# Attention of a DiT block: four key chunks to a group, one PSUM ring, and group sums added in SBUF

## The chip, the cores and the metric

One core of a Trainium2 chip runs the whole program. The metric is device time in microseconds (us), the median of several runs; less is better. Everything is computed in fp32.

## The reference

A transformer block with conditioning, for B = 2 sequences of N = 2048 tokens, C = 576 features, 16 heads of 36:

```python
mod = silu(c) @ w_ada + b_ada                     # six vectors of 576 per sequence
sh_msa, sc_msa, g_msa, sh_mlp, sc_mlp, g_mlp = split(mod, 6, axis=1)
xn = ln(x) * (1 + sc_msa) + sh_msa
q, k, v = (xn @ w_qkv + b_qkv) by head
q, k = ln(q) * qn_g + qn_b, ln(k) * kn_g + kn_b   # over the 36 of a head
o = softmax(q @ k.T * 36**-0.5) @ v
x = x + g_msa * (o @ w_proj + b_proj)
xn2 = ln(x) * (1 + sc_mlp) + sh_mlp
x = x + g_mlp * (gelu(xn2 @ w1 + b1) @ w2 + b2)
```

## The kernel before

For each sequence the program makes q, k and v (`inputs`), runs attention (`attend`) and the output projection (`outputs`); the MLP of both follows. Gains and biases of q and k are measured at run time, and where they are small enough (they are here) the softmax needs no maximum: exp of the scores, a product with v that has a column of ones beside it, and a division by that column's sum.

**A step of attention.** Two heads form a pair (8 pairs, `p`), 512 queries a block (4 blocks, `qb`), and one step (`g`, 8 per block) takes two key chunks of 128: chunk `g` of the first half of the keys and of the second. `scores` (L956) multiplies keys and queries. A head has 36 features; the first 32 lie in `km` and `qm`, in a strip of 32 rows for each of the four (head, half) combinations, which run side by side in TensorE; the last 4 lie in `ke` and `qe`, each four times, split into a high and a low part (`parted`, L761 and L762 on VectorE), and add a second, smaller product in the same strips. Two tiles `s` of two PSUM banks each result, ScalarE takes their exp into `pt` (L960, four buffers), and `values` (L968) multiplies with v: 128 rows by 64 columns, head 0 in one half of the columns and head 1 in the other. The scores of a step are issued ahead of the values of the step before. All of TensorE's instructions stand in the order in which the code is written.

**PSUM.** In attention the eight banks are three `s` tiles and two single-bank `acc` tiles. The values of a query block's eight steps add up in one `acc`.

**The end of a block** (`finish`). VectorE copies `acc` to `ot` (L980). Row 36 of each head holds the denominators: they go to DRAM (`den_dram`, L984) and come back to 64 partitions each (`den`, L985). VectorE takes the reciprocal (L986), multiplies (L987), and two to five DMAs put the result over the queries in `qo` (L992).

**The loads.** `take_q` copies the next block's queries from `qo` to `qm` and `qe`: 4 to 6 and 16 DMAs (L750 and L753, the same lines for keys). In the second block of each pair `take_k` does so for the next pair's keys. All these DMAs are issued by SP, in one queue. In attention the order on SP, ScalarE and VectorE is a scheduler's, which places instructions by its own estimates; what it has placed is fixed when the program is built. Each engine and each queue then goes through its own list in order.

**Hooks** put other work between the steps: the last two token tiles of `inputs`, and for the first sequence the rest of the modulation (`ada_...`).

Of the kernel before, what the change touches and what calls it, by code (L numbers as in the profile page):

```python
# [16 lines left out]
P = 128  # L17
# [14 lines left out]
def dit_block(  # L32
# [165 lines left out]
    def feature_biases(pool, pair, queue):  # L198

        bb = pool.tile([P, PART], F32, name="fb", bufs=1)  # L200
        nc.gpsimd.memset(bb, 0.0)
        for i, r, f, n in row_parts(pair):
            b_j = b_ada[pair[i] * C : (pair[i] + 1) * C]
            queue.dma_start(out=bb[r, n], in_=b_j[f].partition_broadcast(B))
        nc.vector.tensor_scalar_add(bb[0:64, :], bb[0:64, :], 1.0)
        return bb

    def feature_rows(pool, was, bb):
        ps = ada_rows(was)
        rows = pool.tile([P, 384], F32, name="rows", bufs=1)  # L210
        nc.vector.tensor_tensor(rows[:, :PART], ps, bb, ALU.add)
        nc.vector.tensor_tensor(rows[:, PART:], ps[:, 256:PART], bb[:, 256:PART], ALU.add)
        return rows
# [12 lines left out]
    def gates(pool, was, pair, whichs, bias_ins):  # L226

        bb = pool.tile([P, PART], F32, name="bb", bufs=1)
        pb = pool.tile([P, PART], F32, name="pb", bufs=1)
        nc.gpsimd.memset(bb, 0.0)  # L230
        nc.gpsimd.memset(pb, 0.0)
        parts = [*row_parts(pair)]
        for i, r, f, n in parts:
            b_j = b_ada[pair[i] * C : (pair[i] + 1) * C]
            nc.sync.dma_start(out=bb[r, n], in_=b_j[f].partition_broadcast(B))
            nc.sync.dma_start(out=pb[r, n], in_=bias_ins[i][f].partition_broadcast(B))
        ps = ada_rows(was)
        nc.vector.tensor_tensor(bb, ps, bb, ALU.add)
        nc.vector.tensor_tensor(pb, bb, pb, ALU.mult)
        for i, r, f, n in parts:  # L240
            nc.sync.dma_start(out=gate_dram[whichs[i], :, f], in_=bb[r, n])
            nc.sync.dma_start(out=gate_dram[whichs[i] + 1, :, f], in_=pb[r, n])
# [370 lines left out]
    def block_of_any():  # L613
        gains_by_partition()
        with tc.tile_pool(name="ada_later", bufs=2) as ada:
            gates(ada, ada_weights(ada, GATES[0]), *GATES)
            later = feature_biases(ada, LATER[0], nc.sync)
            features(feature_rows(ada, ada_weights(ada, LATER[0]), later), LATER[1])
# [83 lines left out]
    def block_of_small():  # L702
# [40 lines left out]

        def rows_taken(main, ends, halves, first, src, dst):

            for c in halves:
                for h in range(2):
                    r0 = 32 * (2 * c + h)
                    for i, row, d, n in head_rows(first + h * HD, DIMS):
                        nc.sync.dma_start(out=main[r0 + d : r0 + d + n, dst], in_=chunk(i, src(c))[row : row + n, :])  # L750
                    ((i, row, _, n),) = head_rows(first + h * HD + DIMS, HD - DIMS)
                    for j in range(4):
                        nc.sync.dma_start(  # L753
                            out=ends[r0 + n * j : r0 + n * j + n, dst], in_=chunk(i, src(c))[row : row + n, :]
                        )

        def parted(ends, rows, low, sign):

            for a in range(ends.shape[1] // BLK):
                part = ends[rows, a * BLK : (a + 1) * BLK]  # L760
                nc.vector.tensor_scalar(high[rows, :], part, sign[rows, :], None, ALU.mult)  # L761
                nc.vector.scalar_tensor_tensor(  # L762
                    part.bitcast(F32R), part, low[rows, :], high[rows, :].bitcast(F32), ALU.mult, ALU.add
                )

        def take_k(p):
# [3 lines left out]
            parted(e, slice(0, P), low_k, sign_k)  # L770

        def take_k_block(blk):

            c, a = divmod(blk, NBLK // 2)
            dst = slice(a * BLK, (a + 1) * BLK)
            src = lambda c: slice(blk * BLK, (blk + 1) * BLK)
            rows_taken(km[0], ke[0], (c,), C, src, dst)
# [44 lines left out]
        def inputs(b, weights, work, xnt, loaded):  # L822

            wq, wq4, bq = weights
            normed, squares, taken = {}, {}, []

# [33 lines left out]
            def by_feature(t, banks, all_on_vector=False):  # L860
# [17 lines left out]
                if t % TPB == TPB - 1:  # L878
                    if t == TPB - 1:
                        taken.append(take_q(0, 0))  # L880
                    taken.append(take_k_block(t // TPB))
                    if t == NT - 1:
                        taken.pop()()
# [6 lines left out]
            for t in range(NT):  # L890
                both = work.tile([P, 2 * C], F32, name="both", bufs=3)
                for w in range(3):
# [25 lines left out]
                    if w == (1 if t % 2 == 0 else 0):  # L918
                        if t + 1 < NT:
                            ahead = input_by_feature(b, rows)  # L920
                        if t >= 2:
                            by_feature(t - 2, [bank for ps in (s_tile(), s_tile()) for bank in (ps[:, 0], ps[:, 1])])
# [11 lines left out]
            def last(t, spare):  # L934
                ps = s_tile()
                by_feature(t, [spare, ps[:, 0], ps[:, 1]], True)

            return last

        NG = NT // 2  # L940

        def attend(b, pool, hooks):
# [3 lines left out]

            def scores(p, qb, g):
                i, j = p % 2, qb % 2
                keys = slice(g * P, (g + 1) * P)
                tiles = [s_tile() for c in range(2)]  # L950
                for k, q, first in ((km[i], qm[j], True), (ke[i].bitcast(F32R), qe[j].bitcast(F32R), False)):
                    for c in range(2):
                        for h in range(2):
                            r0 = 32 * (2 * c + h)
                            r = slice(r0, r0 + (DIMS if first else 4 * (HD - DIMS)))
                            nc.tensor.matmul(tiles[c][:, h, :], k[r, keys], q[r, :], start=first, stop=not first)  # L956
                pts = []
                for ps in tiles:
                    pt = pool.tile([P, 2, BLK], F32, name="pt", bufs=4)
                    nc.scalar.activation(pt, ps, AF.Exp, scale=SCALE)  # L960
                    pts.append(pt)
                return pts

            def values(p, acc, pts, g):
                for c, pt in enumerate(pts):
                    for h in range(2):
                        v0 = ((g + c * NT // 2) * H + 2 * p + h) * HV
# [4 lines left out]
                            start=(g == 0 and c == 0),  # L972
                            stop=(g == NG - 1 and c == 1),
                        )

            def finish(p, qb, acc):


                ot = pool.tile([P, BLK], F32, name="ot", bufs=2)
                nc.vector.tensor_copy(ot, acc)  # L980
                den = pool.tile([P, BLK], F32, name="den", bufs=2)
# [4 lines left out]
                nc.vector.reciprocal(den, den)  # L986
                nc.vector.tensor_tensor(ot, ot, den, ALU.mult)  # L987
                cols = slice(qb * BLK, (qb + 1) * BLK)
                for h in range(2):
                    for c, row, d, n in head_rows((2 * p + h) * HD):  # L990
                        for r in (row,) if c < FULL else (row, row + 64):
                            nc.sync.dma_start(  # L992
                                out=qo[r : r + n, c, cols], in_=ot[64 * h + d : 64 * h + d + n, :]
                            )

            steps = [(p, qb, g) for p in range(NPAIR) for qb in range(NBLK) for g in range(NG)]
            behind = None
            for p, qb, g in [*steps, (None, None, None)]:
                pts = None if p is None else scores(p, qb, g)
                if (p, qb, g) in hooks:  # L1000
                    hooks[p, qb, g]()
                if g == 3 and (p, qb) != (NPAIR - 1, NBLK - 1):
                    take_q(*((p, qb + 1) if qb + 1 < NBLK else (p + 1, 0)))()
                if g == 4 and qb == 1 and p + 1 < NPAIR:
                    take_k(p + 1)
                if behind is not None:
                    bp, bqb, bg, bpts = behind
                    if bg == 0:
                        acc = acc_tile()
                    values(bp, acc, bpts, bg)  # L1010
                    if bg == NG - 1:
                        finish(bp, bqb, acc)
                behind = (p, qb, g, pts)

# [79 lines left out]
        for b in range(B):  # L1094
# [5 lines left out]
            close_psum()  # L1100
            close_psum = opened_psum(a=2, s=3)
# [4 lines left out]
            def spare_taken():  # L1106
                opening["spare"] = acc_tile()

            def last_inputs_done():
                last_inputs(NT - 1, opening["spare"])  # L1110
                close_work()

            def ada_opened():
                opening["ada"], opening["close"] = opened("ada_later", 2, side="right")
                opening["was"] = ada_weights(opening["ada"], GATES[0])

            def ada_gates():
                gates(opening["ada"], opening["was"], *GATES)
# [10 lines left out]
            def output_opened():  # L1129
# [3 lines left out]
                (0, 0, 0): spare_taken,  # L1133
                (0, 0, 1): lambda: last_inputs(NT - 2, opening["spare"]),
                (0, 0, 2): last_inputs_done,
                (4, 0, 2): output_opened,
            }
            if b == 0:
                hooks |= {
                    (0, 2, 2): ada_opened,  # L1140
                    (1, 0, 4): ada_gates,
                    (2, 0, 4): ada_feature_rows,
                    (2, 0, 6): ada_features,
                }
            attend(b, att, hooks)
            close_att()
            close_psum()
            close_psum = opened_psum(s=4)
# [354 lines left out]
```

## Time and profile before

| | |
|---|---|
| median of 3 runs | 3381.02 us (3376.55 to 3383.67) |
| the profiled execution | 3382.14 us, span 3380.3 us, granted TensorE clock 0.993 |
| attention, first sequence (268 to 1101 us of the span) | TensorE busy 826 of 833, ScalarE 496, VectorE 204 |
| attention, second sequence (1423 to 2244 us) | TensorE busy 817 of 821, ScalarE 494, VectorE 200 |
| L968 values | 4096 instructions, busy 996.2 us |
| L956 scores | 4096 with `qm` and 2048 with `qe`, busy 592.3 and 419.9 us |
| L986 reciprocal | 64, 3353 ns each; idle ahead of them 752.9 us, ended by `den` landing |
| L980 copy | 64, 691 ns each |

A line of the profile names the source line, the engine, the operation and its tiles (out<-in). Matmuls overlap, so their busy times and mean durations are not costs; the distance between starts in the timeline is. An fp32 product appears as two instructions (two passes). For a DMA the profile has the time for which its queue issued it, not its flight; that it has landed shows in who goes on. "Idle before" is the engine's idle time ahead of an instruction, with what ended it.

### The profile page before, as it was taken

To read this page: it belongs to the slowest core of one execution; us is meant where nothing else is said; L and a number is where in the kernel's file an instruction comes from. 1 tells how busy PE (TensorE), PEld (TensorE's weight loads), DVE (VectorE), ACT (ScalarE), POOL (GpSimd) and SP (SyncE) were. 2 spreads that over 40 slices of the span, in tenths; PEclk is the share of its full clock that TensorE was granted. 3 is DMA by queue.
4 is the path that set the end of the run, shared out by engine and by line. 5 is a ranking of instruction groups with operands and counts; after the bars stand their busy time and mean duration, and the time that the engine had idled before them with its cause. 6 is when DMAs were issued, how large, how long until landed. Compare 5 with 4: busy or idle time off the path is not lost.

```text
span 3380.3 us, 46567 instructions
## 1 busy us (share of the span) xinstructions
PE 3318.8 (98%) x18143; PEld 1839.6 (54%) x18143; DVE 1313.8 (39%) x1877; ACT 1439.7 (43%) x1928; POOL 258.8 (8%) x249
## 2 busy tenths in 40 slices
PE   8999999999999999999999999998999999999998
PEld 5773333333333777633333333347888888777776
DVE  4663222222222366612222222226445443544554
ACT  2335555666666033356666666632545453000000
POOL 1110000000000111100000000022000000111111
PEclk9999999999999999999999999999999999999999
DMA  3112212212111401111111111135322222433321
GB/s 125 27 28 60 68 48 61 54 40 52 42 45 35 138 24 29 32 42 42 41 41 38 41 41 43 34 113 184 120 84 83 87 83 75 172 121 116 130 98 36
DMA packets 122996, 234.25 MB, mean 69 GB/s; under 512 B 22279, under 2 KB 64848, under 8 KB 120720
## 3 DMA queue, kind: packets, MB, share of 16 engines
q1 hardware_dynamic: 111800, 193.10, 18.7%
q0 software_dynamic: 10240, 36.61, 3.2%
q8 instruction: 146, 2.39, 0.3%
q10 hardware_dynamic: 728, 1.48, 0.2%
q14 instruction: 82, 0.67, 0.1%
HBM read 125.96 MB, written 56.91 MB: 54 GB/s over the span
## 4 chain that ended last, share of the span: by engine, by line
PE 93%; DVE 2%; issue 2%; SPq 1%; DMA 1%; ACT 1%; POOL 0%; DVEq 0%; POOLq 0%; ACTq 0%
PE acc L968 28%; PE s L956 20%; PE s L1431 14%; PE s L356 13%; PE m L1281 11%; PE m L1295 2%; PE s L367 2%; PE one L1281 2%; SPq L753 1%; PE s L866 1%; PE t L1340 1%; PE s L334 0%; DVE xt L264 0%; DMA wa<-in_w_ada_dram 0%; PE s L182 0%
## 5 line engine op out<-in xcount | busy, mean ns | idle before, releaser
L960 ACT ACTIVATE pt<-s 128x1024 f32<-128x1024 f32 x1024 | 992.6, 1021 | 664.7 <-PE s L956 664.6
L968 PE MATMUL acc<-pt,vt 128*64 128x512 f32 x4096 | 996.2, 607 | 0.0
L956 PE MATMUL s<-qm,km 32*128 32x512 f32 x4096 | 592.3, 641 | 3.6 <-DMA km<-kr 1.4
L968 PEld LDWEIGHTS acc<-pt,vt 128*64 128x64 f32 x4096 | 249.4, 136 | 578.3 <-issue 576.5
L986 DVE RECIPROCAL den<-den 128x512 f32<-128x512 f32 x64 | 214.6, 3353 | 752.9 <-DMA den<-den_dram 752.9
L956 PE MATMUL s<-qe,ke 16*128 16x512 f32 x2048 | 419.9, 789 | 8.2 <-DVE ke L762 5.1
L356 PE MATMUL s<-wq,xnt 128*128 128x288 f32 x1536 | 393.2, 411 | 2.9 <-ACT xnt L342 2.9
L956 PEld LDWEIGHTS s<-qm,km 32*128 32x128 f32 x4096 | 162.4, 183 | 423.6 <-PE acc L968 262.9
L1431 PE MATMUL s<-ws,as 128*128 128x288 f32 x1440 | 351.8, 406 | 0.0
L356 PEld LDWEIGHTS s<-wq,xnt 128*128 128x128 f32 x1536 | 286.5, 191 | 95.1 <-issue 18.5
L1431 PEld LDWEIGHTS s<-ws,as 128*128 128x128 f32 x1440 | 273.6, 190 | 75.6
L980 DVE COPY ot<-acc 128x512 f32<-128x512 f32 x64 | 44.2, 691 | 450.3 <-PE acc L968 450.3
L1281 PE MATMUL m<-s,wb 128*128 128x256 f32 x864 | 211.0, 380 | 4.4 <-DVE s L1255 3.4
L1281 PE MATMUL m<-xnt,wb 128*128 128x256 f32 x864 | 214.7, 385 | 0.0
L1281 PEld LDWEIGHTS m<-s,wb 128*128 128x128 f32 x864 | 164.4, 190 | 27.6 <-DVE s L1255 3.8
L956 PEld LDWEIGHTS s<-qe,ke 16*128 16x128 f32 x2048 | 109.4, 186 | 127.3 <-issue 113.0
L1281 PEld LDWEIGHTS m<-xnt,wb 128*128 128x128 f32 x864 | 159.7, 191 | 33.1 <-issue 12.6
L1431 PE MATMUL s<-ws,hidden 128*128 128x288 f32 x576 | 142.3, 406 | 0.0
L1308 DVE TENSOR_TENSOR cs<-m,cs 128x512 f32<-128x512 f32 x72 | 49.7, 691 | 235.3 <-ACT cs L1307 158.8
L1319 ACT ACTIVATE cs<-cs,b_sb 128x512 f32<-128x512 f32 x144 | 103.9, 722 | 86.8 <-DVE cs L1314 86.8
L1417 DVE TENSOR_TENSOR as<-hidden 128x1152 f32<-128x1152 f32 x80 | 139.4, 1806 | 0.0
L342 ACT ACTIVATE xnt<-s,mod 128x128 f32<-128x128 f32 x180 | 66.8, 460 | 161.6 <-PE s L335 148.3
(149 smaller groups left out, 2364.2 us busy)
## 6 DMA issues: line engine op xcount, KB each, us to landing
gelu<-cs SPq DMA_DIRECT2D x144, 256.0 KB
hidden<-gelu SPq DMA_DIRECT2D x16, 2304.0 KB
qe<-qo SPq DMA_DIRECT2D x1024, 8.0 KB
den<-den_dram SPq DMA_DIRECT2D x128, 128.0 KB
qm<-qo SPq DMA_DIRECT2D x192, 64.0 KB
xr<-x_dram SPq DMA_DIRECT2D x32, 288.0 KB
out_dram<-y POOLq DMA_DIRECT2D x32, 288.0 KB, 3.5
qo<-ot SPq DMA_DIRECT2D x104, 72.0 KB
```

The costliest lines, as they stand in the source:

```text
L342: nc.scalar.activation(dst[:, k, :], t4[:, k * P : (k + 1) * P] if k < FULL else t1[:, :P], AF.Identity, bias=mod[:, which, k, b : b + 1], ...
L356: nc.tensor.matmul(outs[a], stationary(k, a), moving(k, a), start=(first and k == 0), stop=(not first and k == FULL - 1),)
L367: nc.tensor.matmul(outs[a], stationary(FULL, a)[r], moving(FULL, a)[r], start=first, stop=not first)
L956: nc.tensor.matmul(tiles[c][:, h, :], k[r, keys], q[r, :], start=first, stop=not first)
L960: nc.scalar.activation(pt, ps, AF.Exp, scale=SCALE)
L968: nc.tensor.matmul(acc[64 * h : 64 * h + 64, :], vt[:, v0 : v0 + 64], pt[:, h, :], start=(g == 0 and c == 0), stop=(g == NG - 1 and c == 1),)
L986: nc.vector.reciprocal(den, den)
L1281: nc.tensor.matmul(out_m[m], wb[:, slot[m], k, f * P : (f + 1) * P], moving[m](k), start=k == 0 and (m == 1 or (first and m in (2, 5, 6))) ...
L1295: nc.tensor.matmul(out_m[m], w[r, f * P : (f + 1) * P], a[r, FULL, t * PAIR : (t + 1) * PAIR], start=first and m != 4, stop=not first and ...
L1319: nc.scalar.activation(part, part, AF.Gelu, bias=b1_sb[:, g : g + 1])
L1417: nc.vector.tensor_tensor(stationary[m], x_, y_, op)
L1431: nc.tensor.matmul(ms[m], stationary[m][:, f, :], ws[m][:, f, :], start=(f == 0), stop=(f == HF - 1))
```

## The change

A group is now two steps: four key chunks, two rounds of scores (L967) and then eight values products (L981) for the group before. All eight banks form one ring of four `s` tiles, for all stages, and attention no longer opens pools of its own. The values of a group go to one bank of a tile of this ring, and are not carried over groups: VectorE copies the first group's sum of a block to `ot` (L1027) and adds the others to it (L1029). The reciprocal, the product, and the splits of loaded queries and keys are put off by one group each, and VectorE's order in attention is the order of the code. There are five `pt` buffers instead of four and one `den` instead of two. The keys of the last four token tiles are loaded in two pieces, and hooks move to the nearest group.

```diff
+            key_tiles = (0, 4, 8, 12, 14, 16)
+
+            def banks_of_two():
+                return [bank for ps in (s_tile(), s_tile()) for bank in (ps[:, 0], ps[:, 1])]
...
-                if t % TPB == TPB - 1:
-                    if t == TPB - 1:
-                        taken.append(take_q(0, 0))
-                    taken.append(take_k_block(t // TPB))
...
+                if t + 1 in key_tiles:
+                    i = key_tiles.index(t + 1)
+                    taken.append(take_k_block(*key_tiles[i - 1 : i + 1]))
+                return taken
...
-        NG = NT // 2
...
+        NG = NT // 4
...
             def scores(p, qb, g):
                 i, j = p % 2, qb % 2
-                keys = slice(g * P, (g + 1) * P)
-                tiles = [s_tile() for c in range(2)]
...
                 pts = []
-                for ps in tiles:
-                    pt = pool.tile([P, 2, BLK], F32, name="pt", bufs=4)
...
+                for k0 in (2 * g * P, (2 * g + 1) * P):
+                    keys = slice(k0, k0 + P)
+                    tiles = [s_tile() for c in range(2)]
...
+                    for c, ps in enumerate(tiles):
+                        pt = pool.tile([P, 2, BLK], F32, name="pt", bufs=5)
+                        nc.scalar.activation(pt, ps, AF.Exp, scale=SCALE)
+                        pts.append((pt, k0 // P + c * NT // 2))
                 return pts
...
+            def values(p, pts):
+                acc = s_tile()[:, 0, :]
+                for pt, kc in pts:
                     for h in range(2):
...
-                            start=(g == 0 and c == 0),
-                            stop=(g == NG - 1 and c == 1),
+                            start=pt is pts[0][0],
+                            stop=pt is pts[-1][0],
                         )
...
+                return acc
+
+            def finish(p, qb, ot):
...
+                den = pool.tile([P, BLK], F32, name="den")
...
+                def divided():
+                    nc.vector.reciprocal(den, den)
+                    nc.vector.tensor_tensor(ot, ot, den, ALU.mult)
...
+                return divided
...
-                if g == 3 and (p, qb) != (NPAIR - 1, NBLK - 1):
-                    take_q(*((p, qb + 1) if qb + 1 < NBLK else (p + 1, 0)))()
-                if g == 4 and qb == 1 and p + 1 < NPAIR:
-                    take_k(p + 1)
+                due, later = later, []
+                if g == 1 and (p, qb) != (NPAIR - 1, NBLK - 1):
+                    later.append(take_q(*((p, qb + 1) if qb + 1 < NBLK else (p + 1, 0))))
+                if g == 2 and qb == 1 and p + 1 < NPAIR:
+                    later.append(take_k(p + 1))
                 if behind is not None:
                     bp, bqb, bg, bpts = behind
+                    acc = values(bp, bpts)
                     if bg == 0:
-                        acc = acc_tile()
-                    values(bp, acc, bpts, bg)
+                        ot = pool.tile([P, BLK], F32, name="ot", bufs=2)
+                        nc.vector.tensor_copy(ot, acc)
+                    else:
+                        nc.vector.tensor_tensor(ot, acc, ot, ALU.add)
                     if bg == NG - 1:
-                        finish(bp, bqb, acc)
+                        later.append(finish(bp, bqb, ot))
+                if (p, qb, g) in hooks:
+                    later += hooks[p, qb, g]() or []
+                for do in due:
+                    do()
                 behind = (p, qb, g, pts)
...
             att, close_att = opened("att")
-            close_psum()
-            close_psum = opened_psum(a=2, s=3)
...
-            attend(b, att, hooks)
+            with tc.manual_schedule(engines={mybir.EngineType.DVE}):
+                attend(b, att, hooks)
             close_att()
-            close_psum()
-            close_psum = opened_psum(s=4)
```

Beside this, the biases of the gates are loaded in an earlier hook than the gates are computed in (`gate_biases`), and the `+1.0` of `feature_biases` moves to `feature_rows`.

SP's queue is still the scheduler's. As the two programs are built, the issues of three query blocks of an even pair, the first two with key loads, stand so (number of DMAs; `|` is where `den_dram` and `den` begin and end):

```
before  qo 3, qm 1, km 1, qm 1, qe 8, qm 1, qe 3 | den_dram 2, qe 1, qm 1, den 2 | qe 4, ke 2
        qo 3, ke 2, km 1, ke 4, km 1, ke 4, km 1, ke 2, qm 3, qe 12 | den_dram 2, qm 1, qe 1, den 2 | qe 3, ke 2
        qo 2, qm 4, qe 12 | den_dram 2, qe 2, den 2 | qe 2
after   qo 3, qm 1, km 1, qm 1, qe 8, qm 1, qe 4, qm 1, qe 4, ke 2 | den_dram 2, ke 1, den 2 | ke 1, km 1, ke 4, km 1
        qo 3, ke 4, km 1, ke 2, qm 3, qe 12, qm 1, qe 4, ke 2 | den_dram 2, den 2 |
        qo 2, qm 4, qe 16 | den_dram 2, den 2 |
```

## The prediction, made before the changed kernel had run

> **What bounds the kernel now.** I read the page from the top: TensorE is busy 98% of the span, and the chain that ended last is TensorE for 93% of it, led by the values product (L968) and the scores product (L956). A saving on TensorE in attention is a saving in time, as long as nothing else becomes late.
>
> ```profile
> PE 3318.8 (98%) x18143; PEld 1839.6 (54%) x18143; DVE 1313.8 (39%) x1877; ACT 1439.7 (43%) x1928; POOL 258.8 (8%) x249
> ```
>
> Next the timeline of TensorE over one steady attention step (start, us, then what).
>
> ```profile
> 1001.80 1.14 PE L956 MATMUL s<-qm,km 32*128 32x512 f32 x8
> 1002.36 0.82 PE L956 MATMUL s<-qe,ke 16*128 16x512 f32 x4
> 1003.11 1.94 PE L968 MATMUL acc<-pt,vt 128*64 128x512 f32 x8
> 1004.98 1.14 PE L956 MATMUL s<-qm,km 32*128 32x512 f32 x8
> ```
>
> A step lasts 3.18 us (1001.80 to 1004.98), a query block eight of them, 25.4. Its content is smaller. The weight loads of the values stand 0.43 apart (1003.59 and 1004.02 in the same view), so one pass of 512 columns costs 0.43; two passes of `qm` (four strips at once) and four of the values are 6 x 0.43, and the `qe` passes end 0.24 after the `qm` passes (1003.18 against 1002.94). That is 2.82. The missing **0.36 us per step** goes at the two changes between row strips and column halves.
>
> Then I asked what stands just under TensorE. VectorE works only 204 of the 833 us of the first batch's attention, ScalarE 496. But the DMA queue of SP is nearly full. Two answers of the timeline show it, first a query block with nothing else in the queue, then (SP) one that also loads the next pair's keys, then that block's VectorE.
>
> ```profile
> 1081.93 0.52 SPq L984 DMA_DIRECT2D den_dram<-ot  x2
> 1083.13 1.14 SPq L985 DMA_DIRECT2D den<-den_dram  x2
> 1090.72 3.87 SPq L992 DMA_DIRECT2D qo<-ot  x5
> ```
>
> ```profile
> 819.32 2.52 SPq L753 DMA_DIRECT2D ke<-kr  x4
> ...
> 838.86 0.65 SPq L984 DMA_DIRECT2D den_dram<-ot  x2
> 839.56 1.23 SPq L753 DMA_DIRECT2D qe<-qo  x2
> 840.89 1.44 SPq L985 DMA_DIRECT2D den<-den_dram  x2
> ...
> 848.66 2.28 SPq L992 DMA_DIRECT2D qo<-ot  x3
> ```
>
> ```profile
> 827.43 0.69 DVE L980 COPY ot<-acc 128x512 f32<-128x512 f32 x1 [9.09 <-PE acc L968]
> 844.55 3.35 DVE L986 RECIPROCAL den<-den 128x512 f32<-128x512 f32 x1 [16.44 <-DMA den<-den_dram]
> 847.94 0.69 DVE L987 TENSOR_TENSOR ot<-ot,den 128x512 f32<-128x512 f32 x1
> ```
>
> What to see: 30 issues take 819.32 to 838.86, **0.65 us each**, and the round trip of the denominators waits behind them. In the quiet block the product L987 starts at 1090.00, so from `den_dram` to the product is **8.07 us**. The loaded block's reciprocal keeps VectorE idle for 16.44 us. Before the change nobody minds: VectorE has one copy from PSUM per query block, and `acc` has two banks.
>
> [...] here L987 and all behind it do wait for the reciprocal. [...] L992 at 848.66 stands until the product ends at 848.63. [...] TensorE idles 433.74 to 436.41, and the granted clock is 0.50 over 437 to 441.
>
> **The change part by part.**
>
> *Groups of two steps.* One pair of tiling changes goes per group: 2 x 2.82 + 0.36 = 6.0 us instead of 6.35. Unseen in a steady step is the seam `qe` to `qm` within a group; both use row strips, so I take 0; at most it costs the 0.36 that is saved. A query block becomes 24.0, 64 of them 64 x 1.37 = **-88 us** if nothing waits. ScalarE's four exps (1.02 each) fit in 6.0; with five `pt` buffers the second exp of a group waits for the first values of the group before, starts about 3.5 into the group and the fourth ends near 6.5, while its bank is wanted again at 7.3. Cost 0.
>
> *Group sums in SBUF.* One copy and three adds a block instead of one copy: 3 x 0.69 x 64 = 132 us more VectorE, beside TensorE; that alone costs 0. But the bank of a group's sum is one of the ring of four. Five tiles are taken per group, so the fourth score tile of a group needs the bank of the sum taken one group before, that is, the add. It is wanted 1.4 us into the group, and the add normally ends 0.7 after the values. The cover is 0.7 us, and it holds only if VectorE is free.
>
> *VectorE's order pinned.* In the program as built, a block's order is: copy of group 0, **reciprocal and product of the block before**, add of group 1, `qe` split, add, (key split), add. The add of group 1 stands behind the reciprocal, which stands behind the SP queue. And SP's order moved: before, `den_dram` stood ahead of the last 4 to 6 query loads, now it stands behind all of them.
>
> Take T0 as the start of a block's scores. The query loads may start when the scores that last read their buffer end, T0 - 3.6. With N issues ahead of `den_dram`, the add of group 1 ends at T0 - 3.6 + 0.65 N + 8.07 + 0.69 + 0.69. TensorE needs it at T0 + 18.0 + 1.4 = T0 + 19.4. Behind it on VectorE stand the `qe` split of the next block, wanted only at T0 + 24, and the next add; TensorE alone waits for it. The order of SP as built gives N:
> - plain blocks, N = 20 (even pairs of heads) or 22 (odd): ready at 18.9 or 20.2, wait 0 or 0.75;
> - first block with key loads, N = 23 or 24: 20.8 or 21.5, wait 1.4 or 2.05;
> - second such block, N = 29 or 31; in even pairs SP comes free only at T0 - 3.0, after three `qo` of 0.76: 25.3 or 26.0, wait 5.9 or 6.6.
>
> The waits of a pair of heads sum to 7.3 (even) or 10.2 (odd), mean 8.7. A pair takes 96.0 + 8.7 = 104.7 us instead of 101.5. Twelve pairs (1 to 6, both batches) x 3.2 = **+38**. The last pair of a batch loads no keys: three waits of 0.75, 98.3 instead of 101.5, **-6.5** for both. The first pair's key loads wait for no reader and stand early in the queue: four blocks near 24.6, and some 2 us less wait at the opening (TensorE idles there, 287.1 to 289.2, for the last tile's keys): -5 each, **-10**, bounds 0 and -20.
>
> *The clock.* Twelve waits of 6 us are longer than the 2.67 after which the trace shows half clock. It lasted about 6.8 us (granted clock 0.90 over 432.5 to 437, 0.50 to 441, 0.68 to 444, so from 436.1 to 442.9), which is 3.4 us of work. Part of it falls into the wait itself and part is absorbed by the next small waits; I take half, 12 x 1.7 = **+20**, bounds 0 and +41.
>
> *The rest at 0:* ten more key loads per batch by the finer key tiles (6.5 us of SP, under the first groups); the gate biases' DMAs issued earlier and the +1.0 of the features later, inside VectorE's idle time; one `den` buffer instead of two (its reader ends some 20 us before the next load: 1020.6 and 1042); PSUM pools no longer reopened. Each is bounded by a few us either way, in a kernel where one attention block has 25.
>
> Sum: 38 - 6.5 - 10 + 20 = **+41 us** on the profiled execution, which took 3382.1 us (span 3380.3). The median of the runs, 3381.0, stands 1.1 below, so **3422 us**.
>
> **The rivals.**
> - *The queue keeps up: faster.* The place is the second key block, the price its 6 us. An SP instruction itself lasts 0.585 us, and only the gaps make it 0.65; at 0.585 thirty issues give back 2 us, and a round trip 1 us shorter gives another. It decides where the waits of a pair fall under 4 x 1.37 = 5.5 us. Without any wait: 3381 - 88 - 10 = 3283; with half the waits and no half clock: 12 x (4.35 - 5.5) - 9 - 10 = -33, 3348. For it speaks that the blocks before kept up: SP stood idle about 3 us per plain block (1022.2 to 1025.2). Against it: they interleaved, had 25.4 us, and let nothing wait for the reciprocal. Chance 0.12.
> - *It balances:* waits of a pair near 5.5 us, 3375 to 3387. Chance 0.07.
> - *Grouping saves nothing:* the seam costs the full 0.36. Blocks keep 25.4, the add is wanted 1.05 later, the waits per pair fall to about 5.7, and nothing is gained against them: 12 x 5.7 + 20 - 10 = +78, 3459. The shared row strips speak against it. Chance 0.06, within "slower".
> - *The change doesn't do what it says:* excluded for the order of TensorE, which in the program as built has two rounds of scores and then eight values products.
>
> **How the numbers follow.** The likeliest case, the queue behind the reciprocal, has 0.75 and with the rival above it 0.81 for slower. Its own bounds: 0.4 us of round trip more or less per block is about 25 us, the clock 20, the opening 10; 3390 to 3462. Faster has 0.12, of which most lies far below, so the range reaches down to the balanced case only: **3374 to 3462**, leaving out about 0.12 below and 0.06 above. Faster or slower means by over 0.2%, 6.8 us, about what a measurement of this kernel can tell from no change.
>
> **What the profile after would show.** Right: a group of TensorE of 6.0 us in undisturbed stretches; VectorE's reciprocal still waiting for `den`, over 10 us in the second key block; after it TensorE idle about 6 us before `s<-qm` in the last group of that block, released by VectorE's add; attention 20 to 30 us longer per batch; half clock after those waits. Wrong: no wait on the add (the queue kept up, and attention is about 40 us shorter), groups of 6.35 (the seam), or waits on `pt` or on `s` from ScalarE, which I put at 0.

## The result, and the profile after

The changed kernel took 3481.16 us (median of 4 runs, 3479.98 to 3486.48), the kernel before 3382.07 beside it: 1.0299 times as long, 95% interval 1.0281 to 1.0317. It is slower, as forecast, but by 99 us where 41 were forecast, and outside the range. The profiled execution took 3481.4 us, its span is 3479.4, against 3380.3 before: 99.1 us between the two traces that are compared below.

First the row of the score product on the page of the kernel before (busy, mean ns, idle time just before it and what ended most of it); then, from the page of the kernel after, busy time and the rows of the score product, the add and the reciprocal.

```profile
L956 PE MATMUL s<-qm,km 32*128 32x512 f32 x4096 | 592.3, 641 | 3.6 <-DMA km<-kr 1.4
```

```profile
PE 3323.6 (96%) x18143; PEld 1907.6 (55%) x18143; DVE 1458.1 (42%) x2073; ACT 1442.7 (41%) x1928; POOL 256.7 (7%) x249
...
L967 PE MATMUL s<-qm,km 32*128 32x512 f32 x4096 | 617.7, 622 | 87.7 <-DVE ot L1029 83.5
...
L1029 DVE TENSOR_TENSOR ot<-s,ot 128x512 f32<-128x512 f32 x192 | 132.3, 689 | 653.7 <-PE s L981 653.6
...
L1000 DVE RECIPROCAL den<-den 128x512 f32<-128x512 f32 x64 | 214.5, 3351 | 218.3 <-DMA den<-den_dram 218.3
```

The score product was hardly kept waiting before (3.6 us in its row); now it waits 83.5 us for VectorE's add, and the reciprocal idles VectorE 218.3 us for the denominators. Next the timeline of TensorE over one undisturbed group (start, us, then what).

```profile
700.65 1.14 PE L967 MATMUL s<-qm,km 32*128 32x512 f32 x8
701.21 0.81 PE L967 MATMUL s<-qe,ke 16*128 16x512 f32 x4
701.85 1.04 PE L967 MATMUL s<-qm,km 32*128 32x512 f32 x8
702.31 0.81 PE L967 MATMUL s<-qe,ke 16*128 16x512 f32 x4
703.19 3.65 PE L981 MATMUL s<-pt,vt 128*64 128x512 f32 x16
706.77 1.14 PE L967 MATMUL s<-qm,km 32*128 32x512 f32 x8
```

A group lasts 6.12 us (700.65 to 706.77), not the forecast 6.0. Now one of the blocks with key loads, the second of its pair: SyncE's queue (SPq in the lines), then VectorE, then TensorE.

```profile
869.59 2.50 SPq L758 DMA_DIRECT2D qe<-qo  x4
872.14 0.58 SPq L758 DMA_DIRECT2D ke<-kr  x1
873.16 0.51 SPq L996 DMA_DIRECT2D den_dram<-ot  x2
873.71 0.62 SPq L758 DMA_DIRECT2D ke<-kr  x1
874.43 1.16 SPq L997 DMA_DIRECT2D den<-den_dram  x2
```

```profile
870.60 0.69 DVE L1027 COPY ot<-s 128x512 f32<-128x512 f32 x1 [5.43 <-PE s L981]
878.62 3.35 DVE L1000 RECIPROCAL den<-den 128x512 f32<-128x512 f32 x1 [7.33 <-DMA den<-den_dram]
882.01 0.69 DVE L1001 TENSOR_TENSOR ot<-ot,den 128x512 f32<-128x512 f32 x1
882.62 0.68 DVE L1029 TENSOR_TENSOR ot<-s,ot 128x512 f32<-128x512 f32 x1
```

```profile
876.60 1.14 PE L967 MATMUL s<-qm,km 32*128 32x512 f32 x8
877.16 0.81 PE L967 MATMUL s<-qe,ke 16*128 16x512 f32 x4
877.79 1.02 PE L967 MATMUL s<-qm,km 32*128 32x512 f32 x4
883.36 1.22 PE L967 MATMUL s<-qm,km 32*128 32x512 f32 x2 [4.54 <-DVE ot L1029]
...
885.79 6.12 PE L981 MATMUL s<-pt,vt 128*64 128x512 f32 x16
891.84 1.14 PE L967 MATMUL s<-qm,km 32*128 32x512 f32 x8
```

This is the forecast chain link by link: the loads of queries and keys, den_dram behind them at 873.16, the reciprocal at 878.62, product, add, and only then the fourth score tile at 883.36. What was underrated is the last row but one: the values take 6.12 us instead of 3.65. The table of stretches over the same block shows why (from:to, length, busy time and count of PE, PEld, DVE, ACT and POOL, then the granted TensorE clock, the share of the DMA engines and GB/s).

```profile
876.60:880.60 4.00, 2.22 (x18) 0.90 (x16) 1.98 (x1) 1.48 (x2) 0.00 (x0) 1.00 0.16 41
880.60:884.00 3.40, 0.64 (x4) 0.50 (x6) 3.33 (x5) 0.00 (x0) 0.00 (x0) 0.50 0.00 0
884.00:888.00 4.00, 4.00 (x14) 1.11 (x10) 0.48 (x1) 0.13 (x1) 0.00 (x0) 0.50 0.26 63
888.00:891.00 3.00, 3.00 (x10) 0.82 (x8) 0.00 (x0) 1.92 (x2) 0.00 (x0) 0.53 0.14 34
891.80:898.00 6.20, 6.11 (x45) 2.23 (x43) 3.07 (x5) 3.55 (x5) 0.00 (x0) 1.00 0.11 27
```

TensorE has been idle since 878.82; the clock drops to half at 880.56, 1.7 us into the wait, and stays there until 890.80. The group, from 876.60 to 891.84, takes 15.24 us instead of 6.12: 9.12 more, for an idle time of 4.54.

SyncE's queue issued in the order in which the program was built: the second and third row listed for the kernel after stand in the trace one by one, from 960.91 to 985.19 and from 993.36 to 1011.09. In the block shown it issued nothing from 876.95 to 882.73, where `qo` follows the product, which ends at 882.70.

**The sum, by terms.** I measure an attention stage from its first score product to its last values product. Before, the two stages last 837.1 and 825.0 us; after, 894.0 and 872.3: together 104.1 more. Everything else is 5.0 less.

| term, us | forecast | measured | how measured |
|---|---|---|---|
| groups | -88 | -56 | 256 x 6.12 against 512 x 3.17, the mean step on which the forecast's 1.37 us per block rests (its one step of 3.18 is slightly long) |
| TensorE waits, opening included | +109 | +114 | idle stretches over 0.4 us: 90.7 against 10.1; and 33 that is left of the stages |
| half clock | +20 | +47 | 136 us of the stages at clock 0.50, 26 of them idle; half of the other 110 is 55; before, 8.5 |
| outside attention | 0 | -5 | span less stages |
| sum | +41 | +99 | |

The 33 us are a remainder, but the trace shows where they lie. In an undisturbed group the third and the fourth score tile's products run side by side (`x8` at 701.85). Where the add is late, the third tile's run alone (`x4` at 877.79) and the fourth's behind the wait. In the block above the excess is 9.12 us; idle time of 4.54 and half clock (10.2 us recorded from 880.6, 7.4 of it outside the wait, so 3.7) leave 0.9. The same count leaves 0.86 to 0.98 us in 24 of the 25 groups whose counted wait is for the add, 22 us in all 25; and in 14 groups in which the fourth tile comes late by less than the 0.4 us counted here it leaves 0.6 to 1.2, together 12. The forecast counts a wait from the time at which the fourth tile is wanted, so this 0.9 belongs to its waits.

### The profile page after: what moved, and what is told of

It reads as the page before. It is cut to its first block, busy times and chain, and to the rows that moved or that the text cites. A ratio compares the mean times of both kernels' runs of the same rounds, so it can differ in the third digit from the quotient of the medians.

```text
span 3479.4 us, 46882 instructions
## 1 busy us (share of the span) xinstructions
PE 3323.6 (96%) x18143; PEld 1907.6 (55%) x18143; DVE 1458.1 (42%) x2073; ACT 1442.7 (41%) x1928; POOL 256.7 (7%) x249
## 4 chain that ended last, share of the span: by engine, by line
PE 76%; ACT 5%; SPq 5%; DVE 5%; DMA 5%; issue 3%; POOL 0%; DVEq 0%; ACTq 0%; POOLq 0%
PE s L981 22%; PE s L1451 13%; PE s L360 13%; PE m L1301 11%; PE s L967 10%; ACT pt L972 5%; SPq L758 4%; DVE den L1000 3%; DMA den<-den_dram 2%; PE m L1315 2%; PE s L371 2%; PE one L1301 2%; DMA den_dram<-ot 1%; PE s L875 1%; SPq L755 1%
## 5 line engine op out<-in xcount | busy, mean ns | idle before, releaser
L981 PE MATMUL s<-pt,vt 128*64 128x512 f32 x4096 | 973.0, 619 | 16.4
L967 PE MATMUL s<-qm,km 32*128 32x512 f32 x4096 | 617.7, 622 | 87.7 <-DVE ot L1029 83.5
L981 PEld LDWEIGHTS s<-pt,vt 128*64 128x64 f32 x4096 | 280.5, 141 | 649.7 <-issue 501.3
L967 PE MATMUL s<-qe,ke 16*128 16x512 f32 x2048 | 453.1, 790 | 3.7 <-DVE ke L768 3.7
L967 PEld LDWEIGHTS s<-qm,km 32*128 32x128 f32 x4096 | 201.1, 186 | 388.9 <-ACT pt L972 198.7
L1029 DVE TENSOR_TENSOR ot<-s,ot 128x512 f32<-128x512 f32 x192 | 132.3, 689 | 653.7 <-PE s L981 653.6
L1000 DVE RECIPROCAL den<-den 128x512 f32<-128x512 f32 x64 | 214.5, 3351 | 218.3 <-DMA den<-den_dram 218.3
L1027 DVE COPY ot<-s 128x512 f32<-128x512 f32 x64 | 44.2, 691 | 347.0 <-PE s L981 298.1
L967 PEld LDWEIGHTS s<-qe,ke 16*128 16x128 f32 x2048 | 117.7, 187 | 122.8 <-issue 117.4
```

Of the source, the lines that this page charges most:

```text
L981: nc.tensor.matmul(acc[64 * h : 64 * h + 64, :], vt[:, v0 : v0 + 64], pt[:, h, :], start=pt is pts[0][0], stop=pt is pts[-1][0],)
L1029: nc.vector.tensor_tensor(ot, acc, ot, ALU.add)
```

## Theories and experiments

Theory 1: SyncE's queue makes the reciprocal late, VectorE's order passes that on to the add, the ring of banks passes it on to TensorE. Theory H: the idle TensorE falls to half clock, as 1.7 us into the wait above, and this costs more than forecast. Rival A: the queue's length is not it, but the round trip or VectorE's own order. Rivals B and C: the wait only moves, to the query loads or to the keys. Ratios are to the kernel before on the same chip.

### The denominators on another queue (e1_den_pool)

```
-nc.sync.dma_start(out=sums.unsqueeze(0), ...
-nc.sync.dma_start(out=den[64 * h : ...
+nc.gpsimd.dma_start(out=sums.unsqueeze(0), ...
+nc.gpsimd.dma_start(out=den[64 * h : ...
```

> The four DMAs of the denominators (den_dram, den) leave the queue of SyncE for that of GpSimd, which is idle in attention; VectorE's pinned order and all else stay. Theory 1 (the queue of SyncE is what makes the reciprocal late): den_dram goes out as soon as the last add of a block is done, some 7 us into the next block instead of 13 to 20; the reciprocal starts near 12 us, the add of group 1 is never late, the waits of TensorE on VectorE's add (83.5 us) fall under 10, the half clock in attention (136 us of the records) under 30. 3481 minus some 140 to 165: 3316 to 3340 us. Rival A (the round trip and VectorE's own order are too long even on an empty queue, or a DMA issued by GpSimd takes over 8 us longer): waits stay above 50 us, 3450 us or more.

Measured: 3331.5 us, ratio 0.9849 (0.9833 to 0.9866). Four DMAs per block, moved to a queue that is nearly empty in attention (some 15 DMAs over both stages of the kernel after), turn 3% slower into 1.5% faster than before. One block of it, first GpSimd's queue, then VectorE:

```profile
614.79 1.00 POOL L996 DMA_DIRECT2D den_dram<-ot  x2 [5.25 <-DVE ot L1029]
616.64 1.17 POOL L997 DMA_DIRECT2D den<-den_dram  x2 [0.85 <-DMA den_dram<-ot]
```

```profile
619.93 0.69 DVE L1027 COPY ot<-s 128x512 f32<-128x512 f32 x1 [5.43 <-PE s L981]
620.56 3.35 DVE L1000 RECIPROCAL den<-den 128x512 f32<-128x512 f32 x1
623.95 0.69 DVE L1001 TENSOR_TENSOR ot<-ot,den 128x512 f32<-128x512 f32 x1
626.05 0.69 DVE L1029 TENSOR_TENSOR ot<-s,ot 128x512 f32<-128x512 f32 x1 [1.41 <-PE s L981]
```

The reciprocal runs directly behind the copy, and the add waits for TensorE, no longer the other way round. The table of TensorE's waits says the same for the whole run (us, times, longest): after, then e1_den_pool.

```profile
PE s L967 <- DVE ot L1029: 83.5, 26, 9.6
```

```profile
PE s L967 <- DVE ot L1029: 9.5, 6, 4.8
```

Half clock in the stages falls from 136 to 20 us. Rival A is out. Nor is it that GpSimd's DMAs are faster: from `den_dram` to the reciprocal it is 5.46 us in the block of the kernel after (873.16 to 878.62) and 5.77 here (614.79 to 620.56, where the reciprocal also has the copy ahead of it). They start earlier. One of the waits that are left shows the mechanism once more, now on GpSimd's queue:

```profile
786.39 0.99 POOL L996 DMA_DIRECT2D den_dram<-ot  x2 [20.96 <-DVE ot L1029]
792.90 0.56 POOL L1057 DMA_DIRECT2D kr<-in_x_dram  x1 [5.53 <-DMA km<-kr]
793.47 1.06 POOL L997 DMA_DIRECT2D den<-den_dram  x2
```

A residual load that waits for its buffer stands ahead of `den`; the group behind it took 9.1 us too long.

### Only the key loads on another queue (e4_keys_pool)

```
 def take_k(p):
     ...
-    rows_taken(m, e, range(2), C + p * 2 * HD, src, slice(0, N // 2))
+    rows_taken(m, e, range(2), C + p * 2 * HD, src, slice(0, N // 2), nc.gpsimd)
```

> The key loads of the next pair (22 DMAs per pair) go out from GpSimd's queue; the denominators and the rest stay on SyncE. Theory 1: in the two blocks with key loads the number of issues ahead of den_dram falls from 23 to 31 to the 20 to 22 of a plain block; their waits fall from 1.3 to 4.5 us to under 1, no half clock follows, and the last pair's block without key loads shows what is left: 3320 to 3350 us. Rival A (the length of the queue does not matter): 3470 to 3485. Rival C (GpSimd's DMAs are slower and the keys come too late): waits on km or ke, above 3400.

Measured: 3404.8 us, 1.0067 (1.0051 to 1.0084), a miss of over 50 us. The waits on the add fall from 83.5 to 30.8 us, so the keys are most of what makes the reciprocal late. But 22 waits stay, mostly of 0.4 to 2 us, and half clock only falls to 78 us. Waits of 1.35 (at 1571), 1.80 (828) and 1.93 us (932 and 1089) were followed by 3.4 to 6.8 us of it, one of 1.41 (1780) was not. What I got wrong is the price of a short wait, not its cause.

### The reciprocal one group later (e2_late), and VectorE's order not pinned (e3_unpinned)

```
 if bg == NG - 1:
-    later.append(finish(bp, bqb, ot))      # reciprocal behind the copy
+    later2.append(finish(bp, bqb, ot))     # behind the add of group 1
```

> The reciprocal and product of a block are put one group later in VectorE's pinned order, behind the add of group 1 and ahead of the add of group 2; the DMAs stay on SyncE. Theory 1: the reciprocal has 6.1 us more before anything waits behind it. That covers all waits but the longest (7.5 and 9.6 us in the first batch): waits under 15 us, half clock under 35 us, 3320 to 3350 us. Rival A (it is not VectorE's order): 3470 to 3485. Rival B (the later product makes the output DMAs on SyncE's queue later, and with them the query loads behind them, so the wait moves on to qm or qe): waits of TensorE on qm or qe from DMA, 3380 to 3450.

Measured: 3436.5 us, 1.0162 (1.0145 to 1.0179): rival B. TensorE no longer waits for the add of group 1; it waits 52.1 us for the query split (L768 on VectorE), which stands behind the later reciprocal and gets its loads later, since the output DMAs, which wait for the product, stand ahead of them on SyncE's queue: in one block nothing is issued from 800.89 until `qo` at 807.60, and the query loads only from 809.30. Part of the lateness was moved along, not removed.

```
-with tc.manual_schedule(engines={mybir.EngineType.DVE}):
-    attend(b, att, hooks)
+attend(b, att, hooks)
```

> Only the pinned order of VectorE in attention is taken back; in the program as built the reciprocal then stands behind all three adds of a block, and half of the query split ahead of the last add. Theory 1: the reciprocal has some 12 us more, no add waits for it: 3316 to 3350 us, and the whole loss came from grouping and pinning together. Rival A: 3470 to 3485. Rival B: the add behind the query split waits for the query loads instead: 3380 to 3450, waits of VectorE's split on qe from DMA ahead of an add.

Measured: 3907.0 us, 1.1557 (1.1538 to 1.1576). I had expected a gain. VectorE in two blocks of it, then SyncE's queue between them, then the longest wait of that queue's loads in this stretch (us, times, longest):

```profile
940.00 0.48 DVE L767 TENSOR_SCALAR high<-qe,part 128x512 fp32r<-128x512 f32 x1 [11.27 <-DMA qe<-qo]
940.40 0.68 DVE L1029 TENSOR_TENSOR ot<-s,ot 128x512 f32<-128x512 f32 x1
...
973.43 0.49 DVE L767 TENSOR_SCALAR high<-qe,part 128x512 fp32r<-128x512 f32 x1 [11.13 <-DMA qe<-qo]
```

```profile
949.86 1.60 SPq L1006 DMA_DIRECT2D qo<-ot  x2
957.61 2.83 SPq L755 DMA_DIRECT2D qm<-qo  x4
...
969.54 2.48 SPq L758 DMA_DIRECT2D qe<-qo  x4
```

```profile
SPq L755 <- PE s L967: 6.4, 1, 6.4
```

A closed circle: the last add of a block (940.40) stands behind the query split, and that waits for the loads of `qe`. The loads take SyncE from 957.61 to 972.02, and they start only when TensorE's score products have done with the buffer that they fill, for which the queue stands 6.4 us. These products are late because the fourth score tile waits for the add (TensorE idles 4.85 us, to 941.14). Once round is 33.4 us (940.00 to 973.43), and that is the block. The way by `den`, product and `qo` does not hold it up here: `qo` is issued by 951.46. So taking the pin away does not undo the damage; with the order that is then built, the groups on this queue are far worse. (Another pinned order, e2_late, was 45 us better than the kernel after, so the place of the reciprocal does count.) My expectation had looked at the reciprocal's place only and not at what else the add then stands behind.

### Off the queue and one group later (e9_den_late), the residual rows later too (e11_chunks), and the kernel before with the other queue (e10_before_pool)

e9_den_late joins the edits of e1_den_pool and e2_late. e11_chunks is e1_den_pool with

```
-[kr[:, c, a * 640 : a * 640 + C] for c in range(4) for a in range(3)]
+[kr[:, c, a * 640 : a * 640 + C] for c in (2, 3) for a in range(3)]
```

> The denominators on GpSimd's queue and the reciprocal one group later, behind the add of group 1. In e2_late the later product made the query loads late by way of SyncE's queue; with the denominators off that queue the product is only as late as the add, some 6 us later than in e1_den_pool. If what is left in e1_den_pool (waits of 9.5 us on the add, where GpSimd's own loads stand ahead of den) is the add behind the reciprocal: 3318 to 3328. If the output DMAs again push the query loads past the block's end: waits on qe, 3335 to 3400.

> The denominators on GpSimd's queue, and the first residual rows of the output stage go into the last two key chunks only, so that their loads wait on GpSimd's queue from pair 5 on instead of pair 1 on. In e1_den_pool the loads ahead of den cost one wait of some 9 us in the first batch and some smaller ones. If those are what is left: 3318 to 3330; if the output stage then waits for its rows: 3332 to 3345.

Measured: 3336.7 us (0.9871, 0.9852 to 0.9890) and 3336.2 us (0.9869, 0.9853 to 0.9884): neither better than e1_den_pool. With the reciprocal later, waits on the split (13.3 us) take the place of those on the add (9.5). With the residual rows later, the waits on the add stay at 9.0; but the edit did not clear the way, since in the longest of them (5.2 us, at 806.67) a residual load still stands ahead of `den` on GpSimd's queue and waits 5.53 us for its buffer (794.64). What these loads cost is thus not settled. e1_den_pool remains the simplest version, and it beats both kernels.

e10_before_pool makes the edit of e1_den_pool in the kernel before.

> The kernel before, with only the denominators' DMAs on GpSimd's queue. There nothing that TensorE needs stands behind the reciprocal, so theory 1 expects no change: 3376 to 3386 us. If it were faster by tens of us, the gain of e1_den_pool would not be that of the groups.

Measured: 3373.7 us, 0.9989 (0.9980 to 0.9998), a tenth of a per cent, where no change was expected. So the other queue by itself is worth 4 to 5 us, and the groups, with most of the waits gone, some 1.4% more: about 47 us by the two ratios, 42 by the two times, which come from different chips.

### The order of the score rounds (e6_swap_pool)

```
+rounds = rounds if k0 == 2 * g * P else rounds[::-1]    # qm, qe | qe, qm
```

on top of e1_den_pool.

> Two edits on the kernel after: the denominators on GpSimd's queue (as in e1_den_pool, 3331.5 us), and in the second step of a group the 16-row round (qe) goes ahead of the 32-row round (qm), so that a group changes between 32 and 16 rows twice instead of three times. Theory S (the 0.12 us that a group takes over the predicted 6.0 is the seam qe to qm): an undisturbed group falls from 6.12 to about 6.0 us, 256 groups give 25 to 31 us: 3300 to 3307. Rival (the 0.12 comes with the values or with the weight loads, whatever the order): groups stay at 6.12, 3328 to 3336.

Measured: 3356.5 us, 0.9934 (0.9913 to 0.9955). TensorE over one group:

```profile
706.04 1.14 PE L969 MATMUL s<-qm,km 32*128 32x512 f32 x8
706.60 1.05 PE L969 MATMUL s<-qe,ke 16*128 16x512 f32 x8
707.47 1.04 PE L969 MATMUL s<-qm,km 32*128 32x512 f32 x8
708.60 3.65 PE L983 MATMUL s<-pt,vt 128*64 128x512 f32 x16
712.19 1.14 PE L969 MATMUL s<-qm,km 32*128 32x512 f32 x8
```

6.15 us, and 6.12 and 6.13 for the next two, as without the swap: theory S (the 0.12 us over 6.0 is the seam between `qe` and `qm`, and goes with the number of such changes) falls. The second batch's stage is the same too (797.7 us against 799.0 in e1_den_pool). The loss is in the first batch (846.7 against 820.2), where TensorE waits 26.8 us for the add instead of 9.5, in five waits of 2.4 to 7.6 us and two of about 1. That is a later `den` once more. Ahead of the three longest waits (6.1, 6.3 and 7.6 us), residual rows or their products with the gates stand before the last `den` load on GpSimd's queue; in the last of them `den_dram` goes out at 817.71, the product waits for its rows until 821.93, and `den` follows at 823.28. In e1_den_pool one wait is of this kind. So some 20 of the 26.8 us come with the order in which that queue was built, not with the swap itself; the swap also makes TensorE want the fourth score tile earlier, and what that costs was not separated.

### Work into the wait (e8_filled, e15_filled, e14_filled_twice)

```
+again = first and c == 0 and k0 > 2 * g * P and (qb, g) == (1, 3)
+for h in [0, 1] * 5 if again and 0 < p < NPAIR - 1 else []:       # 10 in e14
+    r = slice(32 * h, 32 * h + DIMS)
+    nc.tensor.matmul(tiles[0][:, h, :], k[r, keys], q[r, :], start=True, stop=True)
```

> The kernel after, with TensorE given 4.3 us of repeated work ahead of the last score round of the second block with key loads in pairs 1 to 6 (five pairs of 32-row products into the first score tile, which the right ones then overwrite): 12 places where it idles 2.3 to 9.6 us. Nothing that is late comes earlier. Theory H (idle TensorE falls to half clock, and that costs more than was predicted): the idle time there falls to under 1 us in most places, the half clock of 6.8 to 10.2 us after them (some 95 us of the records) mostly goes: 35 to 45 us of TensorE time less, so 3436 to 3455 although TensorE does 52 us more work. Rival (half clock has another cause, or a wait below 1 us costs as much): 3475 to 3495.

Measured: 3462.9 us, 1.0261 (1.0236 to 1.0286). To compare on one chip, it was run again beside the kernel after (e13_after), with twice the filling as a control.

> The kernel after as it is, beside the filled ones on one chip: 3476 to 3488 us.

> The kernel e8_filled again (five repeated pairs, 4.3 us, in 12 places), in five rounds beside the kernel after on the same chip, because the two earlier ratios (1.0299 and 1.0261) came from different chips and their intervals just meet. Theory H: 10 to 25 us less than the kernel after although TensorE does 52 us more. If the filling only takes the place of idle time and the clock does not matter: the same as after within 4 us, or slower.

> Ten repeated pairs (8.6 us) in the same 12 places: 103 us of added work, some 3 us more per place than TensorE waits there. Control that the repeated work takes the time it should: where it outlasts the wait it must be paid in full. Against five pairs 12 x 4.3 = 52 us more work, of which some 15 us still fall into waits and clock: 3490 to 3515 us. If it stays near 3463, the repeats are cheaper than counted and the filled kernels say nothing about the clock.

| kernel | us | ratio, interval | idle in the stages | half clock in the stages |
|---|---|---|---|---|
| e13_after | 3483.9 | 1.0312 (1.0298 to 1.0326) | 89.7 | 140 |
| e15_filled, repeats 53.5 us | 3467.0 | 1.0251 (1.0234 to 1.0268) | 42.1 | 75 |
| e14_filled_twice, repeats 105.0 us | 3490.6 | 1.0332 (1.0317 to 1.0347) | 33.7 | 34 |

53.5 us of useless work on the engine that bounds the kernel make it 17 us faster: 48 us of idle time are filled, and the half clock loses 21 us less than it did (35 instead of 56). The sum of the three, -15, is close to what the attention stages lose between the two traces (16). Twice as much costs 24 us more than that: of the 51.5 us added, 8 fall into idle time and 18 come back from the clock, so the repeats do take their time. Theory H stands: a wait can be paid twice, once idle and again at half clock. The first run missed its expectation (3436 to 3455): I had counted the clock as saved nearly whole, but waits of 0.5 to 2.6 us and two of 3.5 and 5.1 stay, and half clock follows many of those (granted clock 0.98 and 0.99 over the two stages, against 0.96 in both for the kernel after).

## Why the prediction was right and wrong

- **The bound and the chain: right.** The wait stands where it was put, on the fourth score tile of a block's last group, released by VectorE's add behind the reciprocal, behind den_dram on SyncE's queue. e1_den_pool shows that the queue is the cause.
- **The group, 2 x 2.82 + 0.36 = 6.0 with a seam of 0: a failed term, 31 us.** The group is 6.12. Its scores take 2.54 us (700.65 to 703.19), and the second step of them starts 1.20 after the first, where the sum had 1.10 (two qm passes, 0.86, and 0.24) for a step's scores without a change. So of the 0.36 per step put down to two changes of tiling (by starts in the step before: 0.21 ahead of the values, 0.15 behind them), only 0.22 to 0.24 is saved by a shared one (2 x 3.17 or 3.18, less 6.12), and the seam put at 0 measures some 0.10 (the 0.24 rests on modelled ends). Turning the rounds round changes nothing (e6_swap_pool), so it is not a matter of how often 32 and 16 rows change; why the group takes 0.12 more stays open. The bound was there (0.36), the value taken was its lower end.
- **The waits, 109 us: right in sum, wrong in place.** 114 measured, 81 of them idle time. In quiet pairs (nothing but queries and keys in the queue) TensorE mostly idles 4.1 to 4.9 us in the second key block; with the 0.9 us of products that no longer run side by side this is 5.0 to 5.8, a little under the 5.9 to 6.6 of the forecast. In pairs 1 and 2 of the first batch it idles 9.6 and 7.5 us, because the modulation's weights, gate rows and output weights stand in the same queue; the step "the rest at 0" missed that. That the errors of both kinds nearly cancel in the sum is luck.
- **The half clock, 12 x 1.7 = 20 us: the other failed term, 27 us; 47 measured.** It was counted once per pair, for 6.8 us, half of it absorbed, and the waits of 1.4 to 2.05 us forecast for the first key block were given none. That was my estimate, and no trace showed it; in the trace before, half clock begins at 1443.04, 1.9 us into a wait (TensorE idle 1441.15 to 1444.13, after 0.66 us to 1440.03). In the trace after, 20 of the 21 waits on `s<-qm,km` of 1.17 us or more were followed by half clock of 3.4, 6.8 or 10.2 us, after the first key block too. Filling the waits confirms that the clock is paid on top of the idle time.
- **Right at 0:** `pt` and ScalarE (1.1 us of waits), one `den` buffer, the pinning as such (without it things are worse, e3_unpinned). Outside attention 5 us came back.
- **The marks named for the profile after:** reciprocal waiting over 10 us in the second key block: 6.9 to 7.7 in most quiet pairs, 12.4 in pair 1, so too high; TensorE idle about 6 us: 2.3 to 9.6; attention 20 to 30 us longer per batch: 57 and 47.
- **The rivals.** "The queue keeps up" was put at 3283 without any wait; e1_den_pool comes as near to it as these runs got, at 3331.5, and the difference of 48 us is the group's 0.12 (31 us for 256 groups) and what is left of waits and half clock.

## What to carry to other kernels

When a tuned kernel gets a shorter bounding loop, list what stands in each in-order queue ahead of the new last wait, and move the small round trip that others wait for to a queue of its own, before reordering the engine that waits. Price a wait of the bounding engine above its length, since the clock fell with it: here 1.4 times over all of them (114 + 47 over 114), and twice in the block shown (9.12 over 4.54). Where two products run side by side into two tiles, a late second tile costs their overlap too (0.9 us here), even when the wait itself is too short to see. A constant that is left over when parts are subtracted from a measured step (here 0.36 us) is not yet the price of one thing; take its bound into the middle of the sum.

## What the runs showed of the hardware that was not expected

- A short idle time was enough to slow TensorE. In the attention stages of the kernel after, half clock came in lengths of 3.4, 6.8 and 10.2 us, and already behind waits of 1.17 us (to 2039.85) and 1.35 us (to 1603.00) in a stream that is otherwise busy.
- In the traces of the kernel before and of the kernel after, all changes of the granted clock lie on one grid of 3.4133 us (3413.33 ns), within 5 ns. In the kernel after, half clock begins at 320.78, 433.42, 546.05 and 631.39 us, which are 33, 33 and 25 steps of 3.413 apart. Two waits of 1.73 us each in that kernel, in steps of the grid (length, busy times, then the clock): the first (288.83 to 290.56) falls into two steps and stays without half clock, the second (628.91 to 630.64) falls into one.

```profile
286.66:290.07 3.41, 2.16 (x16) 0.51 (x10) 2.24 (x5) 2.31 (x3) 0.00 (x0) 1.00 0.18 43
290.07:293.48 3.41, 2.92 (x20) 1.58 (x22) 0.43 (x1) 0.01 (x1) 0.00 (x0) 1.00 0.31 66
...
627.99:631.39 3.40, 1.67 (x16) 0.58 (x10) 3.33 (x5) 1.02 (x1) 0.00 (x0) 1.00 0.04 7
631.39:634.80 3.41, 3.41 (x10) 0.77 (x8) 0.38 (x1) 0.33 (x1) 0.24 (x1) 0.50 0.38 94
```

In the two traces, a step of the attention stages at full clock with 1.5 us or more of idle TensorE was followed by half clock in 20 of 20 cases, one with 1.0 to 1.5 us in 2 of 8, one with less in 1 of 925. So in these traces a wait of 1 to 2 us was cheap or dear by where it fell. This is counted from the records; no run moved a wait on purpose.
- In e1_den_pool the DMA round trip on GpSimd's queue was fast enough for all but six of the 64 blocks (though the reciprocal still waits over 1 us for `den` in 15 of them), and each issue takes about 0.5 us there as well (1.00 for two). Of the six waits, only the longest has another load ahead of `den`; for the first block of the first batch the `den` loads took 7.5 us with nothing ahead of them (310.47 to 318.01).
